# A four-layer network on 64x64 images: in the third layer the mode-weight rows are shared by a pair of images, its weights are made during the second layer, and part of the token-by-token scalings become broadcast products on VectorE

## The chip, the cores and the metric

The kernel runs on one core of a Trainium2 chip. The metric is device time in microseconds (us) of one execution. The time before is 8642.2 us, the median of three runs (8638.0 to 8644.23).

## What is computed

The input x is four images of 64 x 64 positions with 128 channels in float32. Four layers follow one another, each as x = x + layer(groupnorm(x)), with 32 groups: a selective scan over two-dimensional paths, a factorized Fourier layer, Fourier attention over the channels as tokens, and neighbourhood attention with a 7 x 7 window. The change is in the third layer. There each of the 128 channels of an image is a token, that is a 64 x 64 plane, and the layer is, cut to what matters:

```python
tokens_norm = instance_norm(tokens)
k = fno_layer(tokens_norm, ...)          # 32 x 32 planes, 16 heads
q = fno_layer(tokens_norm, ...)
v = fno_layer(tokens_norm, ...)          # 64 x 64 planes, 16 heads
attn = softmax(q k / scale) v            # tokens by tokens, in each head
attn = fno_layer(attn, proj)             # the heads back to one plane
attn = instance_norm(attn + tokens)
m = instance_norm(attn)
m = gelu(instance_norm(spectral(m, mixer_w1)) + skip(m))
m = instance_norm(spectral(m, mixer_w2)) + skip(m)
out = instance_norm(m) + attn
```

A `fno_layer` is a spectral convolution (Fourier transform, a weight for each of the low modes, transform back) plus a 1x1 skip. An `instance_norm` takes mean and variance over the plane of one token. The weights are the same for all four images.

## The kernel before

**The order of the network.** `network` (L1584) runs the layers in turn: layer 0 takes about 0 to 6250 us, layer 1 6250 to 6839, layer 2 (the third layer) 6839 to 8017, layer 3 8020 to 8637. Layer 2 begins with `layer2_weights` (L717): some 30 DMAs on the SP and ACT queues (`an`, `quad`, `gram`, `sy`, `bd`, `tok`, `qcol`, `scol`, `scal`, `rows`, ...), about 65 small VectorE operations (the products that make `Wpv`, `mix`, `qk`, `W`, `Wb`), four TensorE transposes `pw`, and stores of the mode weights to a table `wt` in HBM of 32 rows, each of two halves of 8 x 68 numbers. Its scratch tiles lie in a pool of their own, `l2set`.

**Layer 1.** `layer1` (L706) loads its weights (`w1`, `w2` on SP, the rest on ACT) and calls `layer1_image` (L597) for each image: load x in four DMAs of 512 KB, group statistics, along each of the two axes a Fourier transform (`pu`), the mode product (`pg`, copied to `G`), the way back (`pt`, `ph`, copied to `hT`), then a feed-forward network with layer norm on 8 chunks of 512 positions, each stored by the SP queue (L696).

**One image of layer 2**, `layer2_image` (L886). All its operations go through a recorder, so in the profile they carry the recorder's line, L857, and are told apart by the tiles' names. A tile that belongs to one image of a pair carries the parity 0 or 1. Positions are rows (128 partitions x 32 columns of 128 channels). The steps:
- xg: load the image in four chunks, statistics of the group norm (`pg`, `gn_st`), scale and shift it by `so` in four chunks of 128 x 1024, of which GpSimd takes the scale of every second (L1022 to L1029), and store it to a scratch in HBM.
- Statistics of tokens (`token_stats`, L902: 32 bn_stats `in_st` on VectorE, small matmuls `in_pm`), Fourier transform (`dft_y` L950: tiles `pu` and `U`; then `px`, `Xs`), Gram matrix and keys (`pv`, `V`, `pG`, `XG`, `pT`, `TT`, `Z`), scores (`psc`, `Sc`), softmax, and its transpose `pp`, `PT`.
- Skip part: the scratch is read back by token as `ti`, multiplied by a matrix made of the attention (`pk`), stored, and loaded by position as `z` (L1175 to L1210).
- The pz stage (L1213 to L1232): 32 rows of modes. For each row two DMAs, 136 KB each, load `wr`: the row's two halves of the table, each sent to 64 partitions. `WX` = wr times `Xs` of that row (VectorE, or GpSimd for e % 3 = 2), and 8 matmuls with PT add up the heads in `pz`; after 8 rows ScalarE copies pz to `Zp`. `wr` and `WX` have three buffers each.
- `synthesis` (L961): `pa`, copied to `S`, `pb`, added to z.
- Statistics of z, then the mixer: `spectral` (L1257: `pu`, `U`, `pq`, `Zp`, synthesis to `sp`), m = z * A2 by 32 ScalarE operations of 128 x 128, each with its own scale per partition (`affine`, L940); statistics of sp; sp * q1 + f1 again by 32 ScalarE operations and added to m, and gelu (L1288 to L1296); `spectral` again; statistics; sp * q2 (L1303), m = m * scal + sp; statistics of m; the last stage (L1314 to L1322): z * sa + f3 on ScalarE, z + sp on GpSimd (sp is by now the layer's input, loaded again), m * q3 on VectorE, m + z, and the store.

**What sets the order.** `layer2` (L1325) runs two images at a time. `layer2_image` is a generator that yields between steps; `Pace.in_turn` (L865) takes up, each time, the image whose next step can begin first by its own costs of operations (L837), and what it issues is the order of each engine's instructions. DMAs are issued by SP in order. The images of a pair have no common data but the weights; the second begins when the planner finds room, and ends later; when one ends, the third image begins.

Of the kernel before, what the change touches and what calls it, by code (L numbers as in the profile page):

```python
# [10 lines left out]
F32 = mybir.dt.float32  # L11
AF = mybir.ActivationFunctionType
ALU = mybir.AluOpType
# [3 lines left out]
P = 128  # L17
Q = 68
NB = 4
NT = 4096  # L20
DM = 128
# [681 lines left out]
        )  # L703


def layer1(sh, A, x_in, x_out):  # L706
    tc, nc = sh.tc, sh.nc
    with ExitStack() as ctx:
        pool = lambda name, bufs, **kw: ctx.enter_context(tc.tile_pool(name=name, bufs=bufs, **kw))
        wp = pool("l1w", 1)  # L710
        pools = pool("l1big", 2), pool("l1tmp", 2), pool("l1small", 2), pool("l1ps", 4, space=PSUM)
        w = layer1_weights(sh, A, wp)
        for b in range(NB):
            layer1_image(sh, w, pools, x_in(b), x_out(b))


def layer2_weights(sh, A, wp, setup, ps, wt):  # L717
# [109 lines left out]
class Pace:  # L827
# [37 lines left out]
    def in_turn(self, works, together):  # L865

        works, active, now = iter(works), [], 0.0
        while True:  # L870
            while len(active) < together and (g := next(works, None)) is not None:
                active.append([now, now, g])
            if not active:
                return
            a = min(active, key=lambda a: a[0])
            self.t, self.first = a[0], None
            done = next(a[2], None)
            if done is None:
                now = a[1]
                active.remove(a)  # L880
                continue
            a[1] = max(a[1], self.t)
            a[0] = a[1] if done else max(a[0], self.free.get(self.first, 0.0))


def layer2_image(sh, w, pools, x_in, x_out, scr, wt, parity):  # L886

    nc = sh.nc  # L890
    big, tmp, small, ps = pools
    T = [P, NJ, DM]
    C4 = [slice(8 * c, 8 * c + 8) for c in range(4)]
    scal = lambda n: w["scal"][:, n : n + 1]
    tt, ts = nc.vector.tensor_tensor, nc.vector.tensor_scalar
# [44 lines left out]
    def affine(out, src, sc, sf, c):  # L940

        for j in range(8 * c, 8 * c + 8):
            if sf is None:
                nc.scalar.activation(out[:, j, :], src[:, j, :], AF.Copy, scale=sc[:, j : j + 1])
            else:
                nc.scalar.activation(
                    out[:, j, :], src[:, j, :], AF.Identity, scale=sc[:, j : j + 1], bias=sf[:, j : j + 1]
                )

    def dft_y(src):  # L950

# [69 lines left out]
    scr_x, scr_y = scr  # L1021
    for n, c in enumerate(C4):  # L1022
        xc = xg[:, c, :]
        eng = nc.gpsimd if n % 2 else nc.vector
        eng.tensor_tensor(xc, xc, so[:, 0:1, :].to_broadcast([P, 8, DM]), ALU.mult)
        tt(xc, xc, so[:, 1:2, :].to_broadcast([P, 8, DM]), ALU.add)
        rows = slice(1024 * n, 1024 * n + 1024)
        nc.sync.dma_start(scr_x[rows, :].rearrange("(j p) d -> p j d", p=P), xc)
        yield n == 3  # L1029
# [181 lines left out]


    Zp = own([Q, 64, 32], "Zp", tmp)  # L1213
    for g in range(4):
        pz = ps.tile([Q, 8, 64], F32, name="pz", tag="b")
        for e in range(8):
            r = 8 * g + e
            wr = tmp.tile([P, 8, Q], F32, name="wr2", bufs=3)
            for a in range(2):
                nc.sync.dma_start(  # L1220
                    wr[64 * a : 64 * a + 64].rearrange("p h m -> p (h m)"), wt[r, a].partition_broadcast(64)
                )
            WX = tmp.tile([P, 8, Q], F32, name="WX", bufs=3)
            eng = nc.gpsimd if e % 3 == 2 else nc.vector
            eng.tensor_tensor(WX, wr, Xs[:, r : r + 1, :].to_broadcast([P, 8, Q]), ALU.mult)
            for h in range(8):
                nc.tensor.matmul(
                    pz[:, e, :], lhsT=WX[:, h, :], rhs=PT[:, h % 4, h // 4, :], start=(h == 0), stop=(h == 7)
                )
            if e == 7:  # L1230
                nc.scalar.copy(Zp[:, :, 8 * g : 8 * g + 8], pz.rearrange("p r t -> p t r"))
            yield r == 31  # L1232
    ts(Zp[0:1, :, 0], Zp[0:1, :, 0], w["dc"], None, ALU.add)
    yield True
    yield from synthesis(Zp, lambda u, g0, p: tt(at(z, u, g0), at(z, u, g0), p, ALU.add))
# [34 lines left out]
        return sp  # L1270


    sp = yield from spectral(z, w["mix1"])
    m = large("m")
    for c in range(4):
        affine(m, z, A2, None, c)
        yield False
    mu, var = yield from token_stats(sp)
    vs = col("vs")
    tt(vs, A1, A1, ALU.mult)  # L1280
# [6 lines left out]
    yield True  # L1287
    for c in range(5):  # L1288
        if c < 4:
            affine(sp, sp, q1, f1, c)  # L1290
            mc = m[:, C4[c], :]
            tt(mc, mc, sp[:, C4[c], :], ALU.add)
        if c > 0:
            mc = m[:, C4[c - 1], :]
            nc.scalar.activation(mc, mc, AF.Gelu)
        yield c == 4  # L1296
# [4 lines left out]
    q2 = yield from norm_scale(var, 12, "q2")  # L1301
    yield True
    for n, c in enumerate(C4):  # L1303
        affine(sp, sp, q2, None, n)
        stt(m[:, c, :], m[:, c, :], scal(10), sp[:, c, :], ALU.mult, ALU.add)
        nc.sync.dma_start(sp[:, c, :], x_in[1024 * n : 1024 * n + 1024, :].rearrange("(j p) d -> p j d", p=P))
        yield n == 3
# [6 lines left out]
    for n, c in enumerate(C4):  # L1314
        rows = slice(1024 * n, 1024 * n + 1024)
        affine(z, z, sa, f3, n)
        nc.gpsimd.tensor_tensor(z[:, c, :], z[:, c, :], sp[:, c, :], ALU.add)
        tt(m[:, c, :], m[:, c, :], q3[:, c].unsqueeze(2).to_broadcast([P, 8, DM]), ALU.mult)
        yield False
        tt(m[:, c, :], m[:, c, :], z[:, c, :], ALU.add)  # L1320
        nc.sync.dma_start(x_out[rows, :].rearrange("(j p) d -> p j d", p=P), m[:, c, :])
        yield n == 3  # L1322


def layer2(sh, A, x_in, x_out, scr, wt):  # L1325
    tc, nc = sh.tc, sh.nc
    with ExitStack() as ctx:
        pool = lambda name, bufs, **kw: ctx.enter_context(tc.tile_pool(name=name, bufs=bufs, **kw))
        wp = pool("l2w", 1)
        ps = pool("l2ps", 3, space=PSUM)  # L1330
        with tc.tile_pool(name="l2set", bufs=1) as setup:
            w = layer2_weights(sh, A, wp, setup, ps, wt)
        for name, shape in (("XG", [64, 5, P]), ("BD", [P, P])):
            w[name] = [wp.tile(shape, F32, name=f"{name}{n}") for n in range(2)]
            for t in w[name]:
# [5 lines left out]
        paced.nc = Pace(nc)  # L1341
        engines = {mybir.EngineType.PE, mybir.EngineType.Activation, mybir.EngineType.DVE, mybir.EngineType.Pool}
        free = [0, 1]

        def image(b):
            n = free.pop(0)
            yield from layer2_image(paced, w, pools, x_in(b), x_out(b), (scr(n), scr(2 + n)), wt, n)
            free.append(n)

        with tc.manual_schedule(engines=engines):  # L1350
# [233 lines left out]
def network(tc, A, out):  # L1584
    nc = tc.nc
    with ExitStack() as ctx:
# [8 lines left out]
        l0 |= {f"W{n}": dram.tile([4, WD], F32, name=f"l0_W{n}") for n in ("00", "01", "10", "11")}  # L1595
        l0 |= {f"B{n}": dram.tile([NS, CH], F32, name=f"l0_B{n}") for n in range(3)}
        layer0(sh, A, lambda b: A["x"][b], lambda b: x1[b], l0.__getitem__)
        layer1(sh, A, lambda b: x1[b], lambda b: x2[b])
        layer2(sh, A, lambda b: x2[b], lambda b: x3[b], lambda n: scr[n], wt)
        v_pads = [dram.tile([70, 70, DM], F32, name=f"l3_v{n}") for n in range(2)]  # L1600
        layer3(sh, A, lambda b: x3[b], lambda b: out[b], v_pads)

# [181 lines left out]
```

## Time and profile before

| | |
|---|---|
| median of 3 runs | 8642.2 us (8638.0 to 8644.23) |
| the profiled execution's own time | 8638.62 us |
| its span | 8636.8 us |
| mean granted TensorE clock | 0.931 |
| busy share of the span | TensorE 77%, VectorE 79%, ScalarE 74%, GpSimd 64% |
| layer 2: its share | 6839 to 8017 us, some 1180 us |
| in it, busy (sum of the stretches from 6838 to 8018) | TensorE 800 us, VectorE 529, ScalarE 417, GpSimd 154 |
| wr in it | 256 DMAs of 136 KB |

The engines are named PE (TensorE), PEld (its weight loads, which overlap PE), DVE (VectorE), ACT (ScalarE), POOL (GpSimd) and SP (SyncE, which issues DMAs). A row of groups reads: line, engine, operation, out<-in by tile names, shapes, count, then the busy time and the mean of one in ns, and after the bar the idle time of that engine just before them and what ended it ("<-DMA wr<-wt 51.3" is 51.3 us that ended when a wr load landed). A matmul in float32 has two records, so 8 matmuls of pz are 16. A row of the chain of waits is start, duration and the operation; "issue" is time in which the engine waited for nothing that the profile shows. In a table of stretches each engine has its busy time and, in brackets, its instructions; then follow the granted clock of TensorE (1.00 is full), the mean busy share of the 16 DMA engines, and the GB/s that they moved.

### The profile page before, as it was taken

What the parts mean: (1) busy time and instruction counts of PE and PEld (TensorE: products, weight loads), DVE (VectorE), ACT (ScalarE), POOL (GpSimd) and SP (SyncE); (2) the same over time, 40 slices, a digit from 0 to 9 for tenths busy, and PEclk for the clock granted to TensorE, in tenths of its full rate; (3) what the DMA queues carried; (4) which work ended last, traced back from release to release, by engine and by line L of the source; (5) the groups of instructions that cost most, each with busy time, mean ns of one, the idle gap of its engine ahead of it and who ended that gap; (6) DMA issues with size and microseconds to landing.
All of it is one profiled execution on the core that took longest, in us unless ns stands there. A gap on an engine that the chain in (4) does not pass through costs nothing. (4 is left out here: it accounts for less than half of the span.)

```text
span 8636.8 us, 140834 instructions
## 1 busy us (share of the span) xinstructions
PE 6677.0 (77%) x52976; PEld 4227.3 (49%) x52976; DVE 6815.9 (79%) x7900; ACT 6419.2 (74%) x10524; POOL 5540.8 (64%) x2518
## 2 busy tenths in 40 slices
PE   7688888777788777778877777777589677676689
PEld 3344454444444444444544444444377565464456
DVE  2689999998999999899999999999545533534578
ACT  6799999988888898888889989899422114316467
POOL 0689889988888898888889989999400010110233
PEclk9799999999999999999999999999799788787799
DMA  5445555545555454555545445445331131341332
GB/s 109 134 153 170 174 167 167 164 155 160 169 157 181 156 171 153 161 169 157 181 155 174 151 160 171 160 168 175 115 76 39 54 103 54 86 136 30 87 92 78
DMA packets 1292219, 1181.63 MB, mean 137 GB/s; under 512 B 640021, under 2 KB 1077873, under 8 KB 1224594
## 3 DMA queue, kind: packets, MB, share of 16 engines
q1 hardware_dynamic: 1289858, 1170.90, 43.8%
q8 instruction: 417, 6.83, 0.3%
q14 instruction: 264, 2.16, 0.1%
q10 hardware_dynamic: 1680, 1.74, 0.1%
HBM read 980.48 MB, written 189.74 MB: 135 GB/s over the span
## 5 line engine op out<-in xcount | busy, mean ns | idle before, releaser
L476 POOL TENSOR_TENSOR dB<-du,Bb 128x1024 f32<-128x1024 f32 x2048 | 4822.0, 2387 | 670.3 <-DVE h L483 486.5
L483 DVE TENSOR_TENSOR_SCAN h<-dA,state,dB 128x512 f32<-128x512 f32 x4096 | 4955.3, 1268 | 367.7 <-ACT dA L482 264.9
L370 PE MATMUL pt<-ident,h 128*128 128x128 f32 x16384 | 2268.4, 283 | 1071.8 <-ACT hT L380 1065.7
L482 ACT ACTIVATE dA<-delta,A_neg 128x512 f32<-128x512 f32 x4096 | 2748.5, 691 | 211.4 <-DVE h L483 187.4
L370 PEld LDWEIGHTS pt<-ident,h 128*128 128x128 f32 x16384 | 1855.4, 143 | 2121.7 <-ACT hT L380 1868.5
L380 ACT COPY hT<-pt 128x1024 f32<-128x1024 f32 x2048 | 2069.4, 1010 | 192.8 <-PE pt L370 178.7
L405 PE MATMUL yT<-hT,W 128*32 128x256 f32 x16384 | 1403.1, 415 | 2.5 <-DVE y L421 1.9
L206 PE MATMUL cv<-xn,taps 128*128 128x512 f32 x1152 | 623.8, 642 | 17.2 <-DVE e L222 8.8
L405 PEld LDWEIGHTS yT<-hT,W 128*32 128x32 f32 x16384 | 454.2, 150 | 354.5 <-issue 340.0
L857 POOL TENSOR_TENSOR xg<-xg,so 128x1024 f32<-128x1024 f32 x8 | 26.6, 3342 | 690.9 <-ACT so L857 669.9
L1506 POOL TENSOR_TENSOR S<-S,sm 128x784 f32<-128x784 f32 x128 | 191.3, 1495 | 412.6 <-DVE sm L1504 345.5
L316 PE MATMUL dp<-xd,w_dt 65*128 65x512 f32 x512 | 297.8, 664 | 127.8 <-ACT Ct L303 91.4
L325 POOL TENSOR_TENSOR du<-delta,u 128x1024 f32<-128x1024 f32 x128 | 305.2, 2384 | 81.3 <-DVE delta L322 81.3
L857 POOL TENSOR_TENSOR z<-z,sp 128x1024 f32<-128x1024 f32 x16 | 41.8, 2615 | 466.7 <-ACT z L857 466.5
L206 PEld LDWEIGHTS cv<-xn,taps 128*128 128x128 f32 x1152 | 186.4, 191 | 259.1 <-issue 243.8
L297 PE MATMUL xd_ps<-u,w_x 128*48 128x512 f32 x512 | 253.5, 618 | 46.8 <-DMA u<-l_xw 19.1
L1513 ACT ACTIVATE S<-S,mx 128x196 f32<-128x196 f32 x512 | 227.9, 448 | 35.4 <-DVE mx L1540 34.9
L857 PE MATMUL pz<-PT,WX 128*68 128x64 f32 x2048 | 165.9, 246 | 91.7 <-DVE WX L857 74.9
L857 POOL TENSOR_TENSOR WX<-wr,Xs 128x544 f32<-128x544 f32 x32 | 45.9, 1434 | 269.9 <-DMA wr<-wt 242.9
L857 PEld LDWEIGHTS pz<-PT,WX 128*68 128x68 f32 x2048 | 155.6, 160 | 115.5 <-DVE WX L857 76.0
L316 PEld LDWEIGHTS dp<-xd,w_dt 65*128 65x128 f32 x512 | 78.7, 194 | 242.5 <-ACT Ct L303 150.0
L672 ACT ACTIVATE h<-pf,b 128x512 f32<-128x512 f32 x128 | 88.0, 687 | 146.7 <-PE pf L671 146.7
(334 smaller groups left out, 7650.6 us busy)
## 6 DMA issues: line engine op xcount, KB each, us to landing
Bb<-l_B SPq DMA_DIRECT2D x512, 1024.0 KB
W<-l_W SPq DMA_DIRECT2D x512, 256.0 KB
l_y<-y SPq DMA_DIRECT2D x128, 512.0 KB
wr<-wt SPq DMA_DIRECT2D x256, 136.0 KB
u<-l_xw SPq DMA_DIRECT2D x64, 512.0 KB
y<-l_y SPq DMA_DIRECT2D x64, 512.0 KB
u<-l_xr SPq DMA_DIRECT2D x64, 512.0 KB
V<-l_v SPq DMA_DIRECT2D x512, 49.0 KB
```

The costliest lines, as they stand in the source:

```text
L206: nc.tensor.matmul(pm, lhsT=taps[:, s, t, :], rhs=xn[:, dy : dy + 8, dx : dx + 64], start=(t == 0), stop=(t == 8),)
L297: nc.tensor.matmul(xd_ps, lhsT=w_x[:, s, k, :], rhs=u[:, s, :], start=(s == 0), stop=(s == 1))
L316: nc.tensor.matmul(dp, lhsT=w_dt[:, k, s * P : (s + 1) * P], rhs=xd, start=True, stop=True)
L325: nc.gpsimd.tensor_tensor(du, delta, u, ALU.mult)
L370: nc.tensor.transpose(pt[:, j, s, :], G["h"][:, s, t0 : t0 + 32, :].rearrange("p t n -> p (t n)"), sh.ident)
L380: return lambda: nc.scalar.copy(hT, pt.rearrange("p j s d -> p j (s d)"))
L405: nc.tensor.matmul(U["yT"][e][32 * jo : 32 * jo + 32, qo % 2, :], lhsT=U["Ws"][G["g"]][:, :, 4 * q + j], rhs=hT[:, j, :], start=((e, jo) n ...
L476: nc.gpsimd.tensor_tensor(dB, du, B_now[:, q : q + 1, :].to_broadcast([P, 2, CH]), ALU.mult)
L482: nc.scalar.activation(dA, delta[:, s, :], AF.Exp, scale=A_neg[:, k, s, n : n + 1])
L483: nc.vector.tensor_tensor_scan(h[:, s, :, q], dA, dB[:, s, :], state[:, s, n : n + 1], ALU.mult, ALU.add)
L857: r = f(*args, **kw)
L1513: nc.scalar.activation(Sn, Sn, AF.Exp, bias=U["mx"][:, n : n + 1], accum_out=sm[:, n : n + 1])
```

## The change

There are three parts.
- The third layer's weights are made inside the second layer, after its first image is issued, with a scratch pool of their own; the tiles that stay (`l2w`) are now allocated in `network` and live until the end.
- The pz stage is done once for a pair. The image that comes there first leaves its tiles in a list (`beside`) and sleeps: it yields a callable, which `in_turn` asks before it takes the image up again. The second loads each wr row once and makes WX and the matmuls for both, with two tiles pz; GpSimd takes every third of the products of both. Then both images go on from the same time. The wr loads of the layer go from 256 to 128; WX (128 products) and the matmuls of pz stay in number.
- Scalings with a value for each token: a new helper `by_rows` makes a 128 x 1024 product (or sum) on VectorE with the values broadcast along channels. It takes all of m = z * A2 (4 operations in place of 32 on ScalarE, and now ahead of the first `spectral`), and chunks 1 and 3 of the q1, f1 and q2 stages. The scale of xg on GpSimd goes to VectorE; in the last stage GpSimd's z + sp becomes m + sp on VectorE.

The diff, without its empty lines:

```diff
--- before.py
+++ after.py
@@ -703,7 +703,8 @@
         )
-def layer1(sh, A, x_in, x_out):
+def layer1(sh, A, x_in, x_out, l2w, wt):
     tc, nc = sh.tc, sh.nc
     with ExitStack() as ctx:
         pool = lambda name, bufs, **kw: ctx.enter_context(tc.tile_pool(name=name, bufs=bufs, **kw))
@@ -712,6 +713,10 @@
         w = layer1_weights(sh, A, wp)
         for b in range(NB):
             layer1_image(sh, w, pools, x_in(b), x_out(b))
+            if b == 0:
+                setup = pool("l2set", 1)
+                later = layer2_weights(sh, A, l2w, setup, pools[3], wt)
+        return later
 def layer2_weights(sh, A, wp, setup, ps, wt):
@@ -869,10 +874,13 @@
         works, active, now = iter(works), [], 0.0
         while True:
             while len(active) < together and (g := next(works, None)) is not None:
-                active.append([now, now, g])
+                active.append([now, now, g, None])
             if not active:
                 return
-            a = min(active, key=lambda a: a[0])
+            a = min((a for a in active if a[3] is None or a[3]()), key=lambda a: a[0])
+            if a[3]:
+                a[0] = a[1] = max(b[1] for b in active)
+                a[3] = None
             self.t, self.first = a[0], None
             done = next(a[2], None)
             if done is None:
@@ -880,10 +888,14 @@
                 active.remove(a)
                 continue
             a[1] = max(a[1], self.t)
+            if callable(done):
+                a[3] = done
+                continue
             a[0] = a[1] if done else max(a[0], self.free.get(self.first, 0.0))
-def layer2_image(sh, w, pools, x_in, x_out, scr, wt, parity):
+def layer2_image(sh, w, pools, x_in, x_out, scr, wt, parity, beside):
@@ -946,6 +958,10 @@
                 nc.scalar.activation(
                     out[:, j, :], src[:, j, :], AF.Identity, scale=sc[:, j : j + 1], bias=sf[:, j : j + 1]
                 )
+    def by_rows(out, src, v, c, op):
+        tt(out[:, C4[c], :], src[:, C4[c], :], v[:, C4[c]].unsqueeze(2).to_broadcast([P, 8, DM]), op)
     def dft_y(src):
@@ -1021,8 +1037,7 @@
     scr_x, scr_y = scr
     for n, c in enumerate(C4):
         xc = xg[:, c, :]
-        eng = nc.gpsimd if n % 2 else nc.vector
-        eng.tensor_tensor(xc, xc, so[:, 0:1, :].to_broadcast([P, 8, DM]), ALU.mult)
+        tt(xc, xc, so[:, 0:1, :].to_broadcast([P, 8, DM]), ALU.mult)
         tt(xc, xc, so[:, 1:2, :].to_broadcast([P, 8, DM]), ALU.add)
         rows = slice(1024 * n, 1024 * n + 1024)
         nc.sync.dma_start(scr_x[rows, :].rearrange("(j p) d -> p j d", p=P), xc)
@@ -1211,25 +1226,34 @@
     Zp = own([Q, 64, 32], "Zp", tmp)
-    for g in range(4):
-        pz = ps.tile([Q, 8, 64], F32, name="pz", tag="b")
-        for e in range(8):
-            r = 8 * g + e
-            wr = tmp.tile([P, 8, Q], F32, name="wr2", bufs=3)
-            for a in range(2):
-                nc.sync.dma_start(
-                    wr[64 * a : 64 * a + 64].rearrange("p h m -> p (h m)"), wt[r, a].partition_broadcast(64)
-                )
-            WX = tmp.tile([P, 8, Q], F32, name="WX", bufs=3)
-            eng = nc.gpsimd if e % 3 == 2 else nc.vector
-            eng.tensor_tensor(WX, wr, Xs[:, r : r + 1, :].to_broadcast([P, 8, Q]), ALU.mult)
-            for h in range(8):
-                nc.tensor.matmul(
-                    pz[:, e, :], lhsT=WX[:, h, :], rhs=PT[:, h % 4, h // 4, :], start=(h == 0), stop=(h == 7)
-                )
-            if e == 7:
-                nc.scalar.copy(Zp[:, :, 8 * g : 8 * g + 8], pz.rearrange("p r t -> p t r"))
-            yield r == 31
+    beside.append((Xs, PT, Zp))
+    if len(beside) == 1:
+        yield lambda: len(beside) > 2
+    else:
+        for g in range(4):
+            pzs = [ps.tile([Q, 8, 64], F32, name="pz", tag="b") for _ in beside]
+            for e in range(8):
+                r = 8 * g + e
+                wr = tmp.tile([P, 8, Q], F32, name="wr2", bufs=3)
+                for a in range(2):
+                    nc.sync.dma_start(
+                        wr[64 * a : 64 * a + 64].rearrange("p h m -> p (h m)"), wt[r, a].partition_broadcast(64)
+                    )
+                for n, (X, T, _) in enumerate(beside):
+                    WX = tmp.tile([P, 8, Q], F32, name="WX", bufs=3)
+                    eng = nc.gpsimd if (2 * e + n) % 3 == 2 else nc.vector
+                    eng.tensor_tensor(WX, wr, X[:, r : r + 1, :].to_broadcast([P, 8, Q]), ALU.mult)
+                    for h in range(8):
+                        nc.tensor.matmul(
+                            pzs[n][:, e, :], lhsT=WX[:, h, :], rhs=T[:, h % 4, h // 4, :], start=(h == 0), stop=(h == 7)
+                        )
+                if e < 7:
+                    yield False
+            for pz, (_, _, Zn) in zip(pzs, beside):
+                nc.scalar.copy(Zn[:, :, 8 * g : 8 * g + 8], pz.rearrange("p r t -> p t r"))
+            yield g == 3
+        beside.append(None)
     ts(Zp[0:1, :, 0], Zp[0:1, :, 0], w["dc"], None, ALU.add)
     yield True
     yield from synthesis(Zp, lambda u, g0, p: tt(at(z, u, g0), at(z, u, g0), p, ALU.add))
@@ -1270,11 +1294,11 @@
         return sp
-    sp = yield from spectral(z, w["mix1"])
     m = large("m")
     for c in range(4):
-        affine(m, z, A2, None, c)
-        yield False
+        by_rows(m, z, A2, c, ALU.mult)
+    yield False
+    sp = yield from spectral(z, w["mix1"])
     mu, var = yield from token_stats(sp)
     vs = col("vs")
     tt(vs, A1, A1, ALU.mult)
@@ -1287,7 +1311,11 @@
     yield True
     for c in range(5):
         if c < 4:
-            affine(sp, sp, q1, f1, c)
+            if c % 2:
+                by_rows(m, m, f1, c, ALU.add)
+                by_rows(sp, sp, q1, c, ALU.mult)
+            else:
+                affine(sp, sp, q1, f1, c)
             mc = m[:, C4[c], :]
             tt(mc, mc, sp[:, C4[c], :], ALU.add)
         if c > 0:
@@ -1301,7 +1329,10 @@
     q2 = yield from norm_scale(var, 12, "q2")
     yield True
     for n, c in enumerate(C4):
-        affine(sp, sp, q2, None, n)
+        if n % 2:
+            by_rows(sp, sp, q2, n, ALU.mult)
+        else:
+            affine(sp, sp, q2, None, n)
         stt(m[:, c, :], m[:, c, :], scal(10), sp[:, c, :], ALU.mult, ALU.add)
         nc.sync.dma_start(sp[:, c, :], x_in[1024 * n : 1024 * n + 1024, :].rearrange("(j p) d -> p j d", p=P))
         yield n == 3
@@ -1314,22 +1345,19 @@
     for n, c in enumerate(C4):
         rows = slice(1024 * n, 1024 * n + 1024)
         affine(z, z, sa, f3, n)
-        nc.gpsimd.tensor_tensor(z[:, c, :], z[:, c, :], sp[:, c, :], ALU.add)
-        tt(m[:, c, :], m[:, c, :], q3[:, c].unsqueeze(2).to_broadcast([P, 8, DM]), ALU.mult)
+        by_rows(m, m, q3, n, ALU.mult)
+        tt(m[:, c, :], m[:, c, :], sp[:, c, :], ALU.add)
         yield False
         tt(m[:, c, :], m[:, c, :], z[:, c, :], ALU.add)
         nc.sync.dma_start(x_out[rows, :].rearrange("(j p) d -> p j d", p=P), m[:, c, :])
         yield n == 3
-def layer2(sh, A, x_in, x_out, scr, wt):
+def layer2(sh, w, wp, x_in, x_out, scr, wt):
     tc, nc = sh.tc, sh.nc
     with ExitStack() as ctx:
         pool = lambda name, bufs, **kw: ctx.enter_context(tc.tile_pool(name=name, bufs=bufs, **kw))
-        wp = pool("l2w", 1)
         ps = pool("l2ps", 3, space=PSUM)
-        with tc.tile_pool(name="l2set", bufs=1) as setup:
-            w = layer2_weights(sh, A, wp, setup, ps, wt)
         for name, shape in (("XG", [64, 5, P]), ("BD", [P, P])):
             w[name] = [wp.tile(shape, F32, name=f"{name}{n}") for n in range(2)]
             for t in w[name]:
@@ -1341,10 +1369,11 @@
         paced.nc = Pace(nc)
         engines = {mybir.EngineType.PE, mybir.EngineType.Activation, mybir.EngineType.DVE, mybir.EngineType.Pool}
         free = [0, 1]
+        pairs = [[] for _ in range(NB // 2)]
         def image(b):
             n = free.pop(0)
-            yield from layer2_image(paced, w, pools, x_in(b), x_out(b), (scr(n), scr(2 + n)), wt, n)
+            yield from layer2_image(paced, w, pools, x_in(b), x_out(b), (scr(n), scr(2 + n)), wt, n, pairs[b // 2])
             free.append(n)
         with tc.manual_schedule(engines=engines):
@@ -1595,8 +1624,9 @@
         l0 |= {f"W{n}": dram.tile([4, WD], F32, name=f"l0_W{n}") for n in ("00", "01", "10", "11")}
         l0 |= {f"B{n}": dram.tile([NS, CH], F32, name=f"l0_B{n}") for n in range(3)}
         layer0(sh, A, lambda b: A["x"][b], lambda b: x1[b], l0.__getitem__)
-        layer1(sh, A, lambda b: x1[b], lambda b: x2[b])
-        layer2(sh, A, lambda b: x2[b], lambda b: x3[b], lambda n: scr[n], wt)
+        l2w = ctx.enter_context(tc.tile_pool(name="l2w", bufs=1))
+        w2 = layer1(sh, A, lambda b: x1[b], lambda b: x2[b], l2w, wt)
+        layer2(sh, w2, l2w, lambda b: x2[b], lambda b: x3[b], lambda n: scr[n], wt)
         v_pads = [dram.tile([70, 70, DM], F32, name=f"l3_v{n}") for n in range(2)]
         layer3(sh, A, lambda b: x3[b], lambda b: out[b], v_pads)
```

## Prediction

> **What bounds the kernel now.** I first read the chain of waits over the third layer (6838 to 8018 us). The other three layers are almost untouched by the edit.
>
> ```profile
> by line: issue 11.3%; DMA wr<-wt 8.0%; PE pu L857 7.2%; PE pb L857 6.7%; PE pa L857 5.7%; PE pz L857 5.5%; PE px L857 4.8%; ACT sp L857 4.0%; DVE in_st L857 3.5%; SPq L857 3.1%; DVE xg L857 3.0%; PE pv L857 3.0%; PE pG L857 2.8%; DVE m L857
> ```
>
> No engine carries it. TensorE's tiles have the largest sum, but the largest single wait is wr, the mode-weight rows: 8% of 1180 = 94 us. The busy time by stretch gives the stages of the layer's start and of pair 1:
>
> ```profile
> core 0: us, PE busy (x) PEld busy (x) DVE busy (x) ACT busy (x) POOL busy (x), PEclk, DMA share, GB/s
> 6838.00:6874.00 36.00, 0.95 (x4) 0.58 (x4) 15.66 (x66) 0.00 (x0) 0.00 (x0) 0.50 0.38 100
> 6874.00:7036.00 162.00, 121.00 (x808) 98.09 (x808) 82.65 (x161) 31.63 (x61) 33.34 (x33) 0.79 0.29 74
> 7036.00:7195.00 159.00, 112.26 (x1234) 95.12 (x1235) 56.01 (x118) 18.62 (x31) 19.98 (x15) 0.86 0.62 172
> 7195.00:7424.00 229.00, 158.95 (x713) 100.65 (x711) 100.71 (x322) 145.55 (x347) 9.77 (x4) 0.81 0.17 47
> ```
>
> Row 1: 36 us with TensorE idle. Row 3, the pz stage: TensorE idle for 47 of 159 us while the DMA engines are at 0.62. Who TensorE waits for there is in the groups of that stretch:
>
> ```profile
> L857 PE MATMUL pz<-PT,WX 128*68 128x64 f32 x1024 | 80.9, 243 | 46.9 <-DVE WX L857 37.0 <-POOL WX L857 9.0 <-ACT Zp L857 0.8
> L857 DVE TENSOR_TENSOR WX<-wr,Xs 128x544 f32<-128x544 f32 x47 | 35.1, 752 | 53.3 <-DMA wr<-wt 51.3 <-PE pu L857 1.7 <-PE pz L857 0.3
> L857 POOL TENSOR_TENSOR WX<-wr,Xs 128x544 f32<-128x544 f32 x15 | 20.0, 1332 | 136.3 <-DMA wr<-wt 131.8 <-PE pz L857 4.5
> ```
>
> TensorE waits 46 us for WX, and WX for wr. The chain there shows the loop that sets the pace:
>
> ```profile
> 7074.74 10.97 DMA wr<-wt
> 7085.83 0.73 DVE WX L857
> 7086.61 5.70 PE pz L857 x48
> ...
> 7101.95 1.20 PE pz L857 x16
> ```
>
> One row of one image is 16 TensorE records, 1.20 us at best. Behind the 11 us wait three rows took 5.70, or 1.90 a row: PEclk fell. In the undisturbed part the second image's rows came every 1.85 us, a wr loop of about 5.6 us over three buffers.
>
> **The layer's start, moved: -27 us (22 to 29).** The timeline shows the last layer-1 operation and its store, the chain the first layer-2 load:
>
> ```profile
> 6838.06 0.69 DVE L695 TENSOR_TENSOR x<-x,h 128x512 f32<-128x512 f32 x1
> 6839.10 0.46 SPq L696 DMA_DIRECT2D x<-x  x1
> ```
>
> The first xg load is issued at 6869.32, because 30 weight transfers (gram alone 11.9 us) and 15.7 us of VectorE work stand ahead; the first matmul on it is at 6874.5, 5.2 later. With the weights gone, that load waits only for the last store to land (its buffer is taken from layer 1): 6839.1 plus about 2.4 us for 256 KB, as a store at 6249.1 took, is 6841.5, so the first matmul comes at about 6847: -27. Small DMA lane waits give the 22; an earlier landing gives the 29.
>
> **What the move costs layer 1: +5 us (1 to 12).** The weights' DMAs must now pass the same queues. On SP four of them (an, quad, gram, sy) stand before layer 1's first x loads, with waits for gram's lane behind them on ACT's queue. Layer 1 waits at its start for DMA anyway: engines are near full from 6253 to 6292, first matmul at 6269.3. I take +3 (nothing if it hides in that burst, 5 if half of gram's 11.9 shows). The 65 small VectorE operations fall between image 0's first and second axis; seven of 0.6 us among the eight hT copies delay them by about 2 (0 to 4, as there are gaps of 2.4 us between those copies). Four transposes on TensorE, 0.4 us each, add 0 to 1.5. If the DMA cover is thinner than I read it, the upper end is 12.
>
> **Rows shared by a pair: about -44 us a pair.** The row loads go from 256 to 128 (34.8 to 17.4 MB), the products WX and the 2048 pz matmuls stay. Step by step on pair 1:
> - A, the first image, now waits for B. A's last pk ended at 7035.8 and its pz at 7119. In the new order B's score steps and pk stand before all pz. B's psc stood at 7041 before; 21 us from psc to the start and end of pk (as A took from 7014.9 to 7035.8) give about 7062, 7066 with the ti stores' queue. In that time A has nothing: 30 us with little TensorE work.
> - Then 32 rows for both. TensorE needs 2 x 1.20 = 2.40 us a row; the loads need (5.6 + 0.73 for the second WX)/3 = 2.1 us; WX per row is two thirds of two x 0.75 on VectorE and a third of two x 1.33 on GpSimd: 1.0 and 0.9. So TensorE sets the pace, 77 us, plus about 7 for the z loads of B that stand between rows 5 and 6 (before, z and ti cost gaps of 8.8, 10.1 and about 10). End at 7150 against 7194.7: -45. The upper bound of a row is 3.0 us, if VectorE and GpSimd disturb one another as in xg below: +19 a pair; the lower bound is 2.3, with the last clock dips gone: -3.
> - The wait of A behind B, a gain given back, is inside this sum. From here both images run level. Two syntheses take 2 x 17.5 = 35 (to 7186); now both images' statistics of z follow (2 x 6.4 us on VectorE, and 5 for sums and norm) with nothing for TensorE to do: 7205. Two pu, pq and syntheses, 18 + 14 + 35 = 67: 7272. The gelu stage leaves a gap of 5 to 8, and the second spectral step takes the last pb to 7345; before it was at 7382. The tail to the third image's first pg took 42 us and I give it 36, as below: 7381 against 7424.5: -44. Pair 2 the same.
>
> Against levelling speaks a rule of the Trainium skill, "Perfetto Trace Analysis", section Optimization Strategy: "performance may be improved by interleaving those regimes in addition to optimizing within each regime". The trace agrees where the images are out of step: from 7195 to 7272 TensorE was busy 74 of 77 us, since one image's statistics lay under the other's matmuls. By that rule alone the pair would lose the cover: two statistics, gelu stage and tail, some 20 to 30 us. By the row of pz it gains 47 of idle. I count both; the sum above contains 18 us of newly bare statistics.
>
> A second rule weighs on the size: "TensorE: Matmul & The Clock Gate", section What's actually happening, has the clock halved after about 3.4 us of idleness. The rows say 1.90 us for 1.20 after an 11 us wait, and PEclk 0.86 in the stage: three rows cost 2.1 more, so the three long waits of a pair about 6. With the waits gone the rule lets that come back, which the 1.20 in my sum has taken; by the rows' mean as it is (80.9 us for the pair's 64, 1.26 each) a pair would gain 4 less.
>
> **Scalings on VectorE, and GpSimd's part removed: -3 at each start, -5 at each tail.**
>
> ```profile
> L857 DVE TENSOR_TENSOR xg<-xg,so 128x1024 f32<-128x1024 f32 x24 | 41.7, 1760 | 4.7 <-ACT so L857 4.4
> L857 DVE TENSOR_TENSOR m<-m,q 128x1024 f32<-128x1024 f32 x16 | 29.2, 1827 | 0.0
> ...
> L857 POOL TENSOR_TENSOR z<-z,sp 128x1024 f32<-128x1024 f32 x16 | 41.8, 2615 | 466.7 <-ACT z L857 466.5
> L857 POOL TENSOR_TENSOR xg<-xg,so 128x1024 f32<-128x1024 f32 x8 | 26.6, 3342 | 690.9 <-ACT so L857 669.9
> ```
>
> The xg steps on VectorE take 1.22 alone and up to 3.36 beside GpSimd. Four chunks of two at 1.22 are 9.8 us against about 13: -3 a pair (only the image that starts a pair is on the path). In the tail a chunk was 8 ACT scalings (50.0 us for 128 in the groups by form, so 3.1) and a GpSimd add of 2.6 with an m product slowed from 1.22 to 3.37; now it is three VectorE operations (3 x 1.22 = 3.7) beside ACT's 3.1. The last image's tail, 20.6 us from 7996.25 to 8016.87, becomes about 15. The product m = z*A2 (four on VectorE for 32 on ACT, 38.8 us for 128, so 9.7) now stands before pu on VectorE, idle there; q1, f1 and q2 chunks take 24 ACT operations per image to VectorE. The nearest row of a new product is m<-m,q: 1.22 alone, 3.37 beside GpSimd; I take 1.22, for GpSimd has nothing left there. I count these inside the gelu gap and the tail. If VectorE were the later engine, each image's gelu stage would be 5 longer (four products), +10 a pair.
>
> **Sum.** On the profiled run, 8638.62 us with a span of 8636.8: -27 + 5 - 44 - 50 (the second pair carries the last tail and ends about 50 sooner) = -116, or 8523. The median of the runs is 3.6 above the profiled run: 8527.
>
> **Rivals.**
> - Slower: levelling bares everything. If nothing of one image lies under the other's steps, a pair takes TensorE's 392 us (121 + 112 + 159) plus bare stretches of 41 before pz, 30 for A's wait, 7 in pz, 24 for z, 24 for the gelu stage and 64 for statistics, scalings and tail: 190, against 158 idle now. That is +32 a pair, with the start's -22 about +42: 8684. It decides from +11 a pair. Against it: the two images alternate within steps, and VectorE is busy only 101 of 229 us in that stretch. 4 in 100.
> - The rows matter little: what the loads free is taken back by A's wait and the z statistics, and only start and tails are won: -22 + 5 - 2 x 14 = -45, 8597. For it: the windows behind pz hold the larger idle time (70 us of 229), which sharing doesn't touch. 22 in 100.
> - Better packed: level images keep TensorE's clock up (0.76 to 0.81 outside pz), another 20 to 25 a pair: 8480. 16 in 100.
> - The moved loads delay layer 1 by as much as they free, +27 for +5: 8549. For it: layer 1's start is bound by DMA. 10 in 100.
> - As forecast: 8505 to 8550. 48 in 100.
>
> About 0.2%, 17 us, can be told from no change. Chances: 93 faster, 3 within it, 4 slower. The range takes in the forecast, the layer-1 rival and most of the two next to it: 8475 to 8602.
>
> **What would show it.** Right: the first matmul of the layer about 8 us after layer 1's last store; wr x128; pz rows every 2.4 us with TensorE over 0.9 busy and the DMA share near 0.3; the GpSimd groups xg and z gone; the longest new gap, about 13 us, at the statistics of z behind the joint synthesis; layer 1's first matmul at most 5 us later. Wrong: a row of over 3 us with WX as the releaser; A's wait over 35 us; in the stretch behind pz, TensorE idle for over 90 us.

## The result, and the profile after

The changed kernel takes 8526.8 us (8523.1 to 8528.8, 4 runs) beside 8640.1 (8636.5 to 8644.2, 4 runs): a ratio of 0.9868, 95% interval 0.9851 to 0.9885, or -114 us (-99 to -129). The forecast was 8527. The runs below show that the sum came out by luck: two of its terms are off by some 70 us each, in opposite directions.

The profiled execution has a span of 8527.0 us (8528.77 with what lies around it). The stretches of the layer's start and pair 1, up to the third image's first pg, in the table of busy time (columns as in the one of before):

```profile
6859.00:6867.00 8.00, 0.00 (x0) 0.00 (x0) 0.50 (x1) 0.00 (x0) 0.00 (x0) 0.50 0.75 209
6867.00:7046.00 179.00, 135.90 (x930) 109.29 (x931) 87.33 (x180) 37.76 (x70) 23.83 (x29) 0.78 0.40 103
7046.00:7123.00 77.00, 66.75 (x1026) 65.27 (x1024) 38.72 (x44) 5.54 (x10) 27.67 (x19) 0.96 0.51 159
7123.00:7375.00 252.00, 176.24 (x802) 115.29 (x802) 142.79 (x401) 114.56 (x232) 0.00 (x0) 0.82 0.16 43
```

The start is 8 us for 36. The pz stage of both images is 77 us, TensorE busy 67 of it at a clock of 0.96 (before: 112 of 159 at 0.86). Behind it the third image comes 252 us after the end of pz; before it came 229 us after. In the groups of the pz stage the waits for rows are nearly gone:

```profile
L862 PE MATMUL pz<-PT,WX 128*68 128x64 f32 x1024 | 66.4, 228 | 9.9 <-DVE WX L862 9.9
L862 DVE TENSOR_TENSOR WX<-wr,Xs 128x544 f32<-128x544 f32 x42 | 38.3, 930 | 46.3 <-PE pz L862 28.6 <-DMA wr<-wt 17.5
L862 POOL TENSOR_TENSOR WX<-wr,Xs 128x544 f32<-128x544 f32 x19 | 27.7, 1456 | 73.2 <-issue 30.4 <-PE pz L862 21.6 <-DMA wr<-wt 21.2
```

TensorE waits 9.9 us where it waited 46.9, and VectorE now waits most for TensorE (28.6). A row of both images takes 2.4 us in the mean, as forecast; TensorE works for 2.1 of it (66.4 us over 32 rows).

The start in the timeline:

```profile
6858.81 0.69 DVE L695 TENSOR_TENSOR x<-x,h 128x512 f32<-128x512 f32 x1
6859.53 0.36 SPq L696 DMA_DIRECT2D x<-x  x1
6861.93 8.60 SPq L862 DMA_DIRECT2D xg<-x  x6
6867.56 2.79 PE L862 MATMUL pg<-ident,xg 128*128 128x128 f32 x12 [13.92 <-DMA xg<-x]
```

From layer 1's last VectorE operation to layer 2's first matmul it is 8.8 us; it was 36.4: -27.6 for the -27 of the forecast.

By layers, between the same operations in the two profiled executions: layer 0, untouched, ended 8 us later; layer 1 took 602.2 for 589.7 us; the start 8.8 for 36.4; layer 2 from its first matmul to its last m + z 1044.3 for 1141.2 (-97); layer 3, untouched, 6 less. In the profiles of all the kernels here the last VectorE operation of layer 0 starts between 6241 and 6257 us, with the same code, so its 8 us are taken for chance. So are layer 3's 6: from the last m + z to the end it is 611 to 621 us in the same profiles.

### The profile page after: what moved, and what is told of

Same layout as the page of the kernel before. It is cut to its first block, busy times and chain, and to the rows that moved or that the text cites. A ratio compares the mean times of both kernels' runs of the same rounds, so it can differ in the third digit from the quotient of the medians.

```text
span 8527.0 us, 140477 instructions
## 1 busy us (share of the span) xinstructions
PE 6643.2 (78%) x52976; PEld 4210.6 (49%) x52976; DVE 6867.5 (81%) x7956; ACT 6352.6 (74%) x10268; POOL 5488.4 (64%) x2502
## 5 line engine op out<-in xcount | busy, mean ns | idle before, releaser
L206 PE MATMUL cv<-xn,taps 128*128 128x512 f32 x1152 | 622.9, 642 | 17.3 <-DVE e L222 8.8
L1542 ACT ACTIVATE S<-S,mx 128x196 f32<-128x196 f32 x512 | 229.1, 451 | 33.9 <-DVE mx L1569 33.4
L322 DVE SCALAR_TENSOR_TENSOR delta<-delta,dp 128x512 f32<-128x512 f32 x256 | 169.5, 662 | 28.4 <-ACT delta L320 28.4
L319 ACT ACTIVATE delta<-dp 128x512 f32<-128x512 f32 x256 | 152.8, 597 | 52.7 <-PE dp L316 48.7
L256 DVE TENSOR_SCALAR yf<-yf,ln_mv,ln_r 128x256 f32<-128x256 f32 x128 | 169.2, 1368 | 3.2 <-DMA yf<-l_y 3.2
```

The costliest lines, as they stand in the source:

```text
L206: nc.tensor.matmul(pm, lhsT=taps[:, s, t, :], rhs=xn[:, dy : dy + 8, dx : dx + 64], start=(t == 0), stop=(t == 8),)
L1542: nc.scalar.activation(Sn, Sn, AF.Exp, bias=U["mx"][:, n : n + 1], accum_out=sm[:, n : n + 1])
```

## The experiments

All ratios are against runs of the kernel before on the same chip; us are the ratio times 8642.

| kernel | median, us | ratio (95% interval) | us |
|---|---|---|---|
| changed | 8526.8 | 0.9868 (0.9851 to 0.9885) | -114 |
| weights moved alone | 8622.7 | 0.9973 (0.9965 to 0.9982) | -23 |
| rows shared alone | 8644.9 | 0.9998 (0.9990 to 1.0006) | -2 |
| VectorE parts alone | 8554.9 | 0.9898 (0.9884 to 0.9911) | -88 |
| ... of them m alone | 8595.4 | 0.9956 (0.9943 to 0.9968) | -38 |
| ... q and f chunks alone | 8615.1 | 0.9972 (0.9961 to 0.9983) | -24 |
| ... GpSimd's steps alone | 8613.8 | 0.9970 (0.9959 to 0.9981) | -26 |
| changed, not shared | 8530.4 | 0.9876 (0.9863 to 0.9889) | -107 |
| changed, shared, rows loaded for each image | 8621.1 | 0.9977 (0.9966 to 0.9987) | -20 |
| changed, late loads | 8524.3 | 0.9859 (0.9842 to 0.9875) | -122 |
| changed, one image held | 8523.3 | 0.9860 (0.9845 to 0.9875) | -121 |
| changed, second image's pz first | 8484.5 | 0.9819 (0.9804 to 0.9834) | -156 |
| the last and loads behind group statistics | 8484.4 | 0.9814 (0.9801 to 0.9828) | -161 |

**Weights moved alone.** The kernel before with the first part of the diff (`layer1`, `layer2`, `network`).

> The kernel before with the weights' making moved into layer 1 and nothing else. My theory: layer 2's first matmul comes 8.8 us after layer 1's last VectorE operation as in the changed kernel's profile (36.4 before), so -27.6; layer 1 itself takes about 602 us for 590, so +12.5, because the moved loads stand ahead of its x loads; together -15, about 8625. Rival: the 12.5 us and the 8 us by which layer 0 ended later in the changed kernel's profile are chance of that execution; then -27, about 8613.

-23 us (-16 to -30): it lies between the two theories, and the interval takes in the rival's -27. The profiles tell more. In this one layer 1 takes 598.9 us and the start 9.2. Over the six profiles with the loads moved as in the change, layer 1 takes 598.9 to 602.2 us, over the six with the layer as before 589.7 to 591.9. So layer 1's cost is no chance, but it is about 10 us, and the 12.5 of the two first profiles has some chance in it. Layer 2, from its first matmul to its last m + z, took 1154.4 us here for 1141.2 before with the same code in it: single profiles differ by as much as 13 us in this layer.

**Rows shared alone.** The kernel before with `beside`, `in_turn`'s fourth field and the shared loop.

> The kernel before with the pz stage done once for a pair and nothing else. My theory: this is the main gain, the pz stage goes from 159 to about 80 us a pair behind a wait of the first image of about 30, and some of it is given back where the level images have their statistics and gelu stage at the same time; -30 to -40 a pair, -60 to -80 in all, about 8560 to 8580. Rival: without the VectorE products the level images wait for ScalarE's 32 scalings each, and most of the gain is gone: above 8610.

No gain: 0.9998. My theory falls; the rival holds, and further than it said: all of the gain is gone. The pz stage is as fast as in the changed kernel (77 us, TensorE 68 of it), but then the third image comes 290 us after it; before it was 229. The chain there:

```profile
7258.04 16.36 ACT m L857 x56
...
7275.98 6.26 ACT sp L857 x16
...
7291.84 6.26 ACT sp L857 x16
```

ScalarE makes m = z * A2 of both level images in one block, and then sp's scalings of both: the 49 us from 7247 to 7296 have ScalarE busy 44 and TensorE 20.

```profile
7247.00:7296.00 49.00, 19.79 (x82) 13.88 (x79) 16.23 (x62) 44.13 (x116) 0.00 (x0) 0.63 0.00 1
```

**VectorE parts alone.** The kernel before with `by_rows` and its uses, GpSimd's steps gone.

> The kernel before with only the VectorE products and GpSimd's xg and z steps removed. My theory: the start of a pair gains about 7 us (first pu 45.4 us after the first matmul, 52.6 before), the tails about 5 each, so -15 to -25, about 8617 to 8627. Rival: VectorE, now with 24 and 8 operations' work of ScalarE and GpSimd on top, is the later engine where the images overlap, and it is no gain: 8640 or more.

-88 us (-77 to -100), some four times what I expected: both theories fall. So I took the parts singly.

**m alone.**

```diff
-    sp = yield from spectral(z, w["mix1"])
     m = large("m")
     for c in range(4):
-        affine(m, z, A2, None, c)
-        yield False
+        by_rows(m, z, A2, c, ALU.mult)
+    yield False
+    sp = yield from spectral(z, w["mix1"])
```

> The kernel before with one of the VectorE parts alone: m = z*A2 as four VectorE products, ahead of the first spectral step. In the profile of before, ScalarE's m operations stand in the chain of waits among the sp scalings of the other image (12.4 us of m in the 40 us from 7275 on). If ScalarE is what bounds the gelu stage, taking 32 operations of 0.39 us an image away gives 10 to 12 us an image: -30 to -50, about 8600. If VectorE's products only matter at start and tail, as the prediction had it: within 10 us of before.

**q and f chunks alone.**

```diff
-            affine(sp, sp, q1, f1, c)
+            if c % 2:
+                by_rows(m, m, f1, c, ALU.add)
+                by_rows(sp, sp, q1, c, ALU.mult)
+            else:
+                affine(sp, sp, q1, f1, c)
...
-        affine(sp, sp, q2, None, n)
+        if n % 2:
+            by_rows(sp, sp, q2, n, ALU.mult)
+        else:
+            affine(sp, sp, q2, None, n)
```

> The kernel before with another part alone: chunks 1 and 3 of the q1, f1 and q2 stages on VectorE. By the ScalarE theory -5 to -10 an image, -20 to -35 in all, about 8615; by the prediction's, where these were hidden, within 10 us of before.

**GpSimd's steps alone.** The xg scale and the last add, as in the diff.

> The kernel before with GpSimd's two steps alone gone: the scale of xg on VectorE, and m + sp on VectorE in place of z + sp on GpSimd. The prediction gave 3 a pair at the start and 5 a tail: -16, about 8627. Since VectorE's own products beside GpSimd's took 3.3 us for 1.22, it may be twice that, -30; the sum of this run, the m part and the q part should come to the -88 of all three.

The three give -38, -24 and -26, together the -88. m and the q and f chunks come out as the ScalarE theory had them, GpSimd's steps near the larger of the two figures. What m and the chunks relieve stands in the chain of before, in the gelu stage of pair 1:

```profile
7274.75 3.67 ACT sp L857 x9
7278.42 2.33 ACT m L857 x8
7280.76 3.08 ACT sp L857 x8
...
7285.14 3.39 ACT m L857 x9
7288.53 3.08 ACT sp L857 x8
7291.61 3.28 ACT m L857 x9
7294.89 3.08 ACT sp L857 x8
```

One image's scalings of sp alternate with the other's m (an x9 of m is 8 scalings and a gelu), all on ScalarE, one after the other: 7 us of m alone in these 23. (The 12.4 us in the expectation above is more than these lines give: 9.0, gelus included.) The images are out of step here, so one's m delays the other's gelu, and TensorE waits with pu:

```profile
PE pu L857 <- ACT m L857: 14.1, 2, 11.5
```

The run of m alone changes two things, the engine and the place of the products ahead of the first spectral step. No run takes them apart, so how much of the 38 us each is worth is not shown.

**Changed, not shared.** The kernel before with the first and third parts.

> The changed kernel without the sharing: weights moved and VectorE products, each image with its own row loads, images out of step as before. If the parts add up, 8643 - 20 - 88 = 8535, so sharing is worth about -8 to -10 in the changed kernel (8527). If sharing is what the changed kernel lives from once ScalarE is relieved, this is above 8570.

-107 beside -114: the intervals overlap, so by times the sharing is worth nothing that these runs can tell. By the profiles layer 2 is 15 us shorter with it (1044.3 for 1059.5 from first matmul to last m + z), little more than the 13 us between two profiles of the same code.

**Rows loaded for each image.** In the shared loop:

```diff
-                wr = tmp.tile([P, 8, Q], F32, name="wr2", bufs=3)
-                for a in range(2):
-                    nc.sync.dma_start(...)
                 for n, (X, T, _) in enumerate(beside):
+                    wr = tmp.tile([P, 8, Q], F32, name="wr2", bufs=3)
+                    for a in range(2):
+                        nc.sync.dma_start(...)
```

> The changed kernel, but in the shared pz stage each row is loaded once for each image: 256 loads of wr again, order and levelling as in the changed kernel. If the number of row loads is what counts, a row of both images takes two passes of the load loop, 2 x 1.85 = 3.7 us instead of 2.38, and the stage 118 us for 76: +42 a pair, about 8610. If the gain came from doing both images' rows together and from the order, the loads being hidden by two images' matmuls, it stays within 20 us of the changed kernel's 8527.

+94 beside the changed kernel, as the first theory had it. The groups of its pz stage of pair 1, which takes 47 us more:

```profile
L862 PE MATMUL pz<-PT,WX 128*68 128x64 f32 x992 | 79.5, 249 | 42.0 <-POOL WX L862 33.5 <-DVE WX L862 8.2
...
L862 DVE TENSOR_TENSOR WX<-wr,Xs 128x544 f32<-128x544 f32 x42 | 32.0, 766 | 100.8 <-DMA wr<-wt 99.7 <-PE pz L862 1.1
```

The wait for wr is back, and with it TensorE's 42 us of idleness. So the halved loads are worth 94 us to images that run level, and running level, with the wait that makes the images so, costs nearly as much, 87: with rows for each image it is -20 level and -107 out of step.

**Late loads.** Each weight tile is first touched by a copy that needs layer 1's image 0:

```diff
         w[name] = pool.tile(shape, F32, name=name)
+        first = (slice(0, 1),) + (0,) * (len(shape) - 2) + (slice(0, 1),)
+        nc.vector.tensor_copy(w[name][first], after)
         eng.dma_start(w[name], src)
```

> The changed kernel, but each tile of layer 2's weights is touched by a tiny VectorE copy that needs image 0's first finished chunk of layer 1, so that the loads come behind the x loads of images 0 and 1. If layer 1's extra 10 to 12 us come from those loads standing ahead of its x loads, layer 1 is back at 590 to 592 us (602 in the changed kernel) and the time about 8516. If they come from the small VectorE operations and transposes among layer 1's own, it stays at 600 or more, 8527.

-122 us (-108 to -136), which cannot be told from the changed kernel. The first half of my theory holds: from layer 0's last VectorE operation to layer 1's first pu it is again 30.6 us (41.0 in the changed kernel). But layer 1 took 605.5 us: the weights' VectorE operations now fell among the feed-forward chunks of image 0, and the second image's first pu came 15.4 us later than before. The cost moved.

**One image held.** `a[0] = a[1] = max(b[1] for b in active) + 35.0`

> The changed kernel, but the planner takes up the image that slept 35 us (of its own time) later than the other, behind the shared stage; nothing else. If being in step is what costs (16 us of bare z statistics and 21 us before pu of m in the changed kernel's profile), the stretch from the end of pz to the third image's first pg falls from 252 us by 10 to 20 a pair, about 8500. If that time is the work itself, the last image of each pair ends later by the hold and it is slower than 8527.

Inconclusive on its question: in its trace the images stay in step (the pb of both syntheses from 260 to 288 us after the first matmul, 261 to 287 in the changed kernel), so the hold did not do what it was meant to do.

**Second image's pz first.** The shared loop moved ahead of ti, pk and z for the image that makes it; the other sleeps after its z as before:

```diff
+    first = len(beside) == 1
+    if not first:
+        for g in range(4):
+            ...
+        beside.append(None)
     by_token = lambda s: s.rearrange("(s u y) d -> u s (y d)", u=2, y=32)
...
-    if len(beside) == 1:
+    if first:
         yield lambda: len(beside) > 2
```

> The changed kernel, but the second image does the shared pz stage before its own ti, pk and z steps, not after them; nothing else. The first image's wait of 30 us then shrinks to about 8 (pz can start when the second image's PT is there), and the images leave the stage out of step by the second one's pk and z, about 25 us, so that one's statistics lie under the other's matmuls. By the theory that the wait and the levelling eat what sharing gains: -15 to -25 a pair, 8480 to 8500. If the mixer behind pz is bound by the sum of VectorE's and ScalarE's work and not by the level step: within 12 us of 8527.

8484.5 us, 42 below the changed kernel, the intervals apart: faster than both kernels. The first image waits 14 us before pz (30 in the changed kernel, forecast 8), and behind pz the images' pu stand apart again. After the first matmul of the layer, pz of pair 1 now lies from 162 to 238 us (179 to 255 in the changed kernel), and the third image's first pg at 486 (507). The gain of 21 a pair is almost all the wait before pz, 17 us; the stretch behind, 248 us for 252, now also holds the second image's pk.

**The last with loads behind image 0's group statistics.** The copy above takes its value from image 0's statistics.

> The pz_first kernel, with the loads of layer 2's weights held behind image 0's group statistics (each tile touched by a tiny VectorE copy that needs them) and so behind its x loads, while the VectorE operations on the weights stay between image 0's two axes. In late_loads layer 1's start was back (30.6 us from layer 0's end to the first pu, 41.0 in the changed kernel), but the weights' VectorE operations fell into the feed-forward chunks and took 11 us there. If those two are the parts of layer 1's extra 12 us, here it keeps the start's 10 without paying in the chunks: layer 1 at 592 to 595, about 8475. If the operations between the axes now wait for loads that come later, layer 1 stays at 600 and the time at pz_first's 8484.

Layer 1 does what the first theory said: 592.5 us. But the time is 8484.4, as without it. The intervals, -161 (-149 to -172) and -156 (-143 to -169), rule out neither theory. In the profile layer 2 took 1016.8 us for 1003.8. One stretch of the same work shows at least where, first pz_first, then this kernel:

```profile
7220.00:7285.00 65.00, 50.72 (x233) 32.91 (x234) 35.26 (x96) 38.49 (x71) 0.00 (x0) 0.84 0.00 1
```

```profile
7213.00:7278.00 65.00, 50.85 (x196) 33.11 (x195) 31.73 (x89) 34.71 (x63) 0.00 (x0) 0.68 0.00 1
```

TensorE is busy as long but gets through 196 records for 233, at a granted clock of 0.68 for 0.84. Why the clock is lower there stays open. It need not be so in every execution: one of the five, at a mean clock of 0.939, took 8470.6 us, the profiled one, at 0.936, 8486.5.

## Why the prediction was right in its time and wrong in its split

**The layer's start, -27**: right, -27.6.

**Layer 1, +5**: 12.5 in this pair of profiles and about 10 over all of them, at the upper end of its 1 to 12. The term that failed is the x loads, +3 ("nothing if it hides in that burst"): the first pu after layer 0 came at 41.0 us for 30.6, +10.4. What the operations between the axes and the transposes cost is too small to read: the second axis's pu came 33.9 us behind the first for 30.9, but 31.6 to 33.3 in the other profiles with the layer as before. In the timeline of the changed kernel:

```profile
6258.05 0.51 SPq L728 DMA_DIRECT2D gram<-in_c_gram  x1
...
6260.16 9.89 SPq L581 DMA_DIRECT2D w<-in_w  x2
...
6270.47 17.26 SPq L701 DMA_DIRECT2D x<-x  x4
...
6288.14 6.65 PE L58 MATMUL gn_ps<-ident,x 128*128 128x128 f32 x32 [31.54 <-DMA vib<-in_vib]
```

and of the kernel before:

```profile
6260.16 8.50 SPq L701 DMA_DIRECT2D x<-x  x4
6269.26 4.65 PE L58 MATMUL gn_ps<-ident,x 128*128 128x128 f32 x24 [20.89 <-DMA c_sy<-in_c_sy]
```

The issue of w1, w2 now lasts 9.9 us (0.8 before), for w2 waits 9.2 us until the load of `b`, one of layer 1's small ones, has landed. The x loads behind it are issued over 17.3 us (8.5 before). The DMA engines were 0.83 busy before from 6248 to 6269, so the start was bound by DMA, and the new loads did not hide in it.

**Rows shared, -44 a pair**: this step failed. (Six of the 44 are the tail's.) Its first half came out, in part by luck. A's wait was 30 us as said, and a row of both took 2.4 us (77 us for the stage, forecast 84), but not because "TensorE needs 2 x 1.20". The 1.20 is a row that stands alone; rows that follow one another take 1.02 in the changed kernel,

```profile
7083.58 25.49 PE pz L862 x400
```

and some 1.06 before, where three did so at full clock. TensorE's 2.1 us a row of both and its waits of 9.9 us in the stage make up the 2.4. So two of the signs for being right did not come: TensorE was 0.87 busy, not over 0.9, and the DMA share was 0.51, not near 0.3.

Its second half, "level" with a gelu gap of 5 to 8 and 36 to the third image, was too short: TensorE's wait before pu of m is 19.4 us,

```profile
PE in_pm L862 <- DVE in_st L862: 19.4, 1, 19.4
```

since the sums of B's statistics are queued ahead of A's pu on TensorE, and those statistics ran on VectorE in turn with A's products; and the tail is 47 us from the last pb to the third image's first pg. From the last pb of the first spectral step to that of the second it took 94 us where the text had 73; with the tail that is 32 us more than in the sum. A front 31 us earlier happened to balance it: pz ended 20 us sooner (a first pk 12 earlier, of which the sum had nothing, and pz 8 shorter), and the syntheses, statistics and first spectral step took 11 less.

What sharing is worth by itself is the comparison without it. There B's pz ends at 314 us after the first matmul and A's at 232; with it both end at 255. The third image waits for A's end, about 13 us before its first pg, and A's last m + z came at 494 for 499. So the 59 us that B gained brought the third image hardly sooner. Of the -94 of the two pairs in the sum the sharing had some -78, the tails the rest; it measured -2 alone and -7 beside the changed kernel without it. The rule of the Trainium skill, "Perfetto Trace Analysis", Optimization Strategy, on interleaving was the one to weigh more: with the same 256 row loads, the run out of step is 87 us faster than the level one.

**Scalings on VectorE, -3 a start and -5 a tail**: this step failed too, -16 said and -88 measured. The tail was right (33 us before from the last m * scal + sp to the last m + z, 27 after). The start was worth about 12 up to the first pk (140 us after the first matmul for 152; in the run with GpSimd's steps alone gone also 140), and the sum had left out even the 3. The larger error is the sentence "I count these inside the gelu gap and the tail": the m product and the q, f chunks, which I gave nothing of their own, are 62 us. The profile of before had shown it: ScalarE busy 45 of 53 us from 7272 to 7325 with TensorE at 27.

```profile
7272.00:7325.00 53.00, 27.32 (x109) 18.81 (x107) 19.12 (x56) 44.98 (x106) 0.00 (x0) 0.68 0.00 0
```

The second rule, the clock gate, held in its direction: the clock in the pz stage went from 0.86 to 0.96. Its size was not right: TensorE's busy time in pz fell from 80.9 to 66.4 us, 14.5 where the text had some 6. How much of it is the clock, and how much that rows now follow one another, is not shown.

Of the rivals, "the rows matter little" had the cause nearly right for the sharing, but missed the ScalarE part, and with it its time, 8597.

## What to carry to other kernels

A sum that comes out right says little on its parts: run each part alone. A scaling per token as one broadcast product on an idle VectorE, in place of many small ScalarE operations, is worth its share of the chain wherever those stand between two images' steps, and this is read in the chain, not in the engines' busy shares. Sharing a load between two works removes the load's wait and adds a meeting point: ask what the first does while it waits, and what then runs bare in both at once; here letting the second image do the shared stage before its own other steps gave 42 us more.

## What was not expected of the hardware

VectorE's WX products were slower in the shared stage: 930 ns in the mean for 752, GpSimd's 1456 for 1332. The slowing comes with the two engines working at the same time: in the changed kernel's stage for pair 1 the 18 VectorE products that ran clear of any of GpSimd's took 711 to 727 ns, the other 24 up to 1860. With the same split at the slower pace of rows loaded for each image the means are 766 and 1329. It cost little here: of TensorE's 9.9 us of waiting for WX, 7.8 are one wait, behind a row still loading. Untouched layers differ by several us from one execution to the next (layer 0's end over 15 us in fourteen profiles), so that a layer's time from one profile is not to be read closer than that.
